# Count loads from GpSimd's queue, work moved out of the output attention's preparation, and first missing-edge tiles loaded ahead of a branch

## The chip, the cores and the metric

The kernel runs on 1 core of one Trainium2 chip. Its time is the device time of one execution, in microseconds (us); three runs of the kernel before took 2191.27, 2193.19 and 2195.49 us, median 2193.19 us. Engines are named as the profile names them: PE multiplies matrices, DVE is the vector engine, ACT the scalar engine with its function tables, POOL is GpSimd, and SP issues transfers. Each engine runs its own instructions in the order that was fixed when the program was built. A transfer that SP or POOL issues waits in that engine's order too (the profile writes SPq, POOLq).

## The reference

Four graph layers run one after the other on 4096 nodes of 64 features with a dense 0/1 adjacency of 4096 x 4096. Each layer gets the normalised, rectified features `h` and adds its output to `x`.

```
# layer 0: eight attention heads, then one "output attention" over their joined result
e_o   = leaky_relu(o1[:, None] + o2[None, :], 0.2)
att_o = softmax(where(mask, e_o, -9e15));   out = tanh(att_o @ Who)
# layer 1: hyperbolic attention, for every pair of nodes
adj_att = sigmoid(left[:, None] + right[None, :] + b) * adj
support = einsum('ij,ijd->id', adj_att, logmap(x_i, x_j))
# layer 2: mean over neighbours, a dense layer, rows scaled to length 1
# layer 3: the last 100 neighbours of each row, with weights 0.5 ** (number of neighbours behind)
rank = cumsum(adj != 0, axis=1);  w = mask * where(pos > 0, 0.5 ** (k - pos), 0);  out = w @ support + bias
```

## The kernel before, in words

Nodes are 32 blocks of 128 (`NB` = 32, `P` = 128). The adjacency is held as one byte per edge in DRAM (`mask_d`), written once from the float input during the attention heads, and loaded again by each later stage. The stages, with their place in the profiled execution:

- **Heads** (to about 937 us). Each of 8 heads runs over 2 halves of the targets. At the end of heads 3 and 7, `finish_unit` (from line 1660) goes over four groups: four transposes into PSUM, a copy by ACT into a slot of `h` (`hT`, line 1714), eight small products (L1720), an addition into `who` by DVE (L1731). All four groups use one slot, `by_g[:, 3]`. `h` and `by_g` are the same memory.
- **Output attention, preparation** (about 950 to 985 us). First constants of layer 1 are made (lines 1743 to 1768: three small loads by POOL and 11 instructions of one column on DVE), and POOL clears the tile `MOV` (L1777, 128 x 4096 bf16), of which later three rows are filled from DRAM (L1868). Then maxima of `who` are reduced (L1918 to L1935), joined over partitions by POOL (`omax`, L1166), and from these the value tiles `YB`, `YC`, `YD` are made. The sum over nodes, `wsum` (L1985, on DVE), feeds the mean value, and the last instruction of the preparation is `prepared` (L2006). Most of this stands in `in_order()`, which keeps DVE, ACT and PE in the order of the program text.
- **Output attention, four units u of 1024 targets** (to 1184 us). For each of 8 values of q, SP loads a mask tile `mo` (L2074, 512 KB, 3 buffers), DVE writes its complement and POOL stores it to DRAM (`noedge`, L2079), ACT takes signs (L1200), DVE forms the masked tiles B and C (L1206, L1214), and PE multiplies them (L2097). From u = 1 on, DVE also works on layer 1's nodes of the unit before.
- **A branch** (L2192, `values_load`) that sends unusual data to a slow path. What stands inside the branch isn't mixed with what stands ahead of it.
- **Pairs of layer 1** (about 1206 to 1785 us). `weights_of` (from line 2217) loads a tile `nm` of missing edges (L2221, 256 KB, 4 buffers), PE multiplies it (L2228) and then `MOV` (L2231), ACT takes the sigmoid. PE forms distances (L2259) in between.
- **Layer 2** (about 1785 to 1945 us). Two halves of 8 mask tiles `m2` (L2623, 1 MB, 3 buffers); POOL also copies `cat` (L2578) for each group of 512 nodes.
- **Layer 3** (about 1945 to 2185 us). Four units u; for each of 8 values of q a mask tile `m3` (L2690, 512 KB, 3 buffers), of which each of 4 blocks goes through PE (L2697, L2705), ACT (L2714) and PE again (L2679). A unit's sums are copied out of PSUM (L2724), half by DVE and half by ACT, before the next unit's sums may start. POOL stores the output (L2739).

Beside these runs a check of the input that is spread over the stages: `count_odd` (line 946) loads 1 MB of the float adjacency into a tile `raw` (L949, 2 buffers) and counts on DVE the entries that are neither 0 nor 1 (L950). It is called 64 times: 16 times in the output attention (q = 0, 2, 4, 6 of each unit), 11 times in layer 2, and 37 times in layer 3 (12, 9, 8 and 8 in its units). All 64 loads are issued by SP, in one queue with `mo`, `m2` and `m3`. A load waits in SP's order for its `raw` buffer, and what stands behind it on SP waits with it.

The order on each engine comes from a scheduler that goes by priorities in the order of the program text and by its own estimate of when things are ready. It may move a load or a count ahead of other work. `issue_after` and `behind` keep what is in their block behind a given instruction. The measured order shows that a `raw` load is not held by them (two were issued at 937 and 953 us, ahead of `prepared` at 980 us); the count on DVE is.

Of the kernel before, what the change touches and what calls it, by code (L numbers as in the profile page):

```python
# [9 lines left out]
F32 = mybir.dt.float32  # L10
BF16 = mybir.dt.bfloat16
# [5 lines left out]
U8 = mybir.dt.uint8  # L17
AF = mybir.ActivationFunctionType
ALU = mybir.AluOpType
AX = mybir.AxisListType  # L20
# [4 lines left out]
P = 128  # L25
N = 4096
NB = N // P
D = 64
G = 512
NG = N // G  # L30
GB = G // P
# [7 lines left out]
PROJ_EPS = 0.004  # L39
# [12 lines left out]
HW = N // 2  # L52
NS = HW // G
# [777 lines left out]
def kernel(  # L831
# [24 lines left out]
    nc = tc.nc  # L856
    NH, F, O = W_sp.shape[0] + W_int.shape[0], W_sp.shape[1], W_sp.shape[2]
# [10 lines left out]
    ctx = ExitStack()  # L868
# [74 lines left out]

        return col.unsqueeze(2).to_broadcast([P, col.shape[1], width])

    def count_odd(pool, c):

        raw = pool.tile([P, HW], F32, name="raw", tag="raw", bufs=2)
        nc.sync.dma_start(raw, adjT[c % NB * P : (c % NB + 1) * P, c // NB * HW : (c // NB + 1) * HW])  # L949
        nc.vector.scalar_tensor_tensor(  # L950
            raw, raw, 0.0, raw, ALU.is_gt, ALU.not_equal, accum_out=bad[:, c : c + 1]
        )
# [83 lines left out]
    with ExitStack() as l0:  # L1036
# [403 lines left out]
        with ExitStack() as ha:  # L1440
# [34 lines left out]
            for hf in range(2):  # L1475
# [9 lines left out]
                for hd in range(NH):  # L1485
# [174 lines left out]
                    def finish_unit(hf=hf, hd=hd, ev=ev, fme=fme):  # L1660
# [50 lines left out]
                            return  # L1711
                        c = hd // 4
                        for bq in range(NS):
                            hT = by_g[:, 3]
                            transpose_to(
                                hT, [num[:, bq * GB + b, :] for b in range(GB)], P, ps, nc.scalar.copy
                            )
                            pw = ps.tile([P, GB, D + 2], F32, name="pwho", tag="misc")
                            for b in range(GB):
                                nc.tensor.matmul(  # L1720
                                    pw[:, b, :],
                                    lhsT=hT[:, b * P : (b + 1) * P],
                                    rhs=rho[:, c, :],
                                    start=True,
                                    stop=True,
                                )
# [13 lines left out]
        lq = ctx.enter_context(tc.tile_pool(name="l1", bufs=1))  # L1740
        KA = D + 2

        def scalar_tile(name):
            return lq.tile([P, 1], F32, name=name)
# [4 lines left out]
        nc.vector.reciprocal(sqc, rabs)  # L1749
        nc.vector.tensor_tensor(cc, rt, rt, ALU.mult)  # L1750
        nc.vector.reciprocal(cc, cc)
        c2, m2c, p2c, m4c, cneg, maxn, hrow = (
            scalar_tile(n) for n in ("c2", "m2c", "p2c", "m4c", "cneg", "maxn", "hrow")
        )
        nc.vector.tensor_tensor(c2, cc, cc, ALU.mult)
        nc.vector.tensor_scalar(m2c, cc, -2.0, None, ALU.mult)
        nc.vector.tensor_scalar(m4c, cc, -4.0, None, ALU.mult)
        nc.vector.tensor_scalar(p2c, cc, 2.0, None, ALU.mult)
        nc.vector.tensor_scalar(cneg, cc, -1.0, None, ALU.mult)
        nc.vector.tensor_scalar(maxn, rabs, 1.0 - PROJ_EPS, None, ALU.mult)  # L1760
        nc.vector.tensor_scalar(hrow, rabs, 0.5, None, ALU.mult)
        wab = lq.tile([P, 2, D], F32, name="wab")
        nc.gpsimd.dma_start(
            wab.rearrange("p s d -> p (s d)"),
            w_att.rearrange("k o -> (k o)").unsqueeze(0).to_broadcast([P, 2 * D]),
        )
        bt = scalar_tile("bt")
# [9 lines left out]
        nc.gpsimd.memset(MOV, 0.0)  # L1777

        def layer1_nodes(bs, work, augs):

# [93 lines left out]
        with ExitStack() as ob:  # L1874
# [42 lines left out]
            for i, bs in enumerate(halves):  # L1917
                nc.vector.tensor_reduce(mx[:, i, 0:1], tcol[:, bs], AX.X, ALU.max)  # L1918
                nc.vector.tensor_reduce(mx[:, i, 1:2], tcol[:, bs], AX.X, ALU.min)
                nc.vector.tensor_reduce(mx[:, i, 2:3], vals[:, bs], AX.XY, ALU.max)  # L1920
                nc.vector.tensor_reduce(mx[:, i, 3:4], vals[:, bs], AX.XY, ALU.min)
            with in_order():

                pr = ps.tile([NB, P], F32, name="pro", tag="misc")
# [60 lines left out]
                nc.vector.tensor_reduce(wsum, vals.rearrange("p b d -> p d b"), AX.X, ALU.add)  # L1985
# [24 lines left out]
                None,  # L2010
                ALU.mult,
            )

            def finish_unit(u, evs):

# [44 lines left out]
            for u in range(4):  # L2060
# [133 lines left out]
    def pairs_fast(es, VT):  # L2194
# [10 lines left out]
        with ExitStack() as ss:  # L2205
# [11 lines left out]
            def weights_of(src, tgt):  # L2217


                nm = work.tile([P, GB, G], U8, name="nm", tag="nm", bufs=4)  # L2220
                nc.sync.dma_start(  # L2221
                    nm, noedge_d[src][tgt // NS][:, :, (tgt % NS) * G : (tgt % NS + 1) * G]
                )
# [237 lines left out]
    def layers_fast(es, wide, *sums):  # L2461
# [211 lines left out]
        for u in range(4):  # L2673
# [14 lines left out]
            for q in range(NQ):  # L2688
                m = work.tile([P, JT, HO2], U8, name="m3", tag="m3", bufs=3)
                nc.sync.dma_start(m, mask_d[q][u // 2][:, :, hs])  # L2690
                for t in range(JT):
# [142 lines left out]
```

## Time and profile before

| what | value |
|---|---|
| runs | 2191.27, 2193.19, 2195.49 us; median 2193.19 us |
| profiled execution | 2194.35 us; its span 2192.6 us |
| mean granted clock of PE | 0.933 |
| busy | PE 1923.9 us, DVE 1765.8, ACT 1623.2, POOL 84.7 |
| counts (L950) | 64 x about 2.29 us on DVE, 70.2 us of DVE idle time ahead of them, waiting for `raw` |
| `raw` loads | 64 x 1024 KB, median 6.6 us from issue to landing |

The profiled execution stands 1.2 us above the median of the runs. A row of a table by stage gives the stretch, its length, for each engine its busy time and (x the number of instructions), then the clock granted to PE as a share of full speed, the mean busy share of the 16 DMA engines, and the GB/s that they moved. A line of a timeline gives start, length, engine, line, operation, output <- input with shapes, and in brackets how long the engine had been idle and what ended that. A line of waits gives who waited, at which line, for whom, the total, how often, and the longest.

### The profile page before, as it was taken

Reading aid. Unit: us, or ns where it says so; the run is one execution under the profiler, and the core shown is the slowest. Engines: PE = TensorE matmul, PEld = TensorE weight load, DVE = VectorE, ACT = ScalarE, POOL = GpSimd, SP = SyncE. Lnnn points to the kernel's source line nnn. Section 1 sums busy time; section 2 is a strip of 40 time slices with the busy share of each in tenths; the row PEclk is TensorE's granted clock in tenths of the full one; section 3 lists DMA queues with packets and bytes.
Section 4 is the critical chain, followed back from the end, with each engine's and each line's share of the span. In section 5 each row is a group of like instructions: output and inputs, shape, how many; then the busy total and the mean of one; then the engine's idle time right before and its main releaser. Section 6 shows DMA issues by size and latency. Waiting matters only on the chain.

```text
span 2192.6 us, 43992 instructions
## 1 busy us (share of the span) xinstructions
PE 1923.9 (88%) x19276; PEld 865.5 (39%) x19276; DVE 1765.8 (81%) x2330; ACT 1623.2 (74%) x1402; POOL 84.7 (4%) x124
## 2 busy tenths in 40 slices
PE   4989989999999999949997699999999968989878
PEld 3444444444444444423443233333333323444222
DVE  6689989997898899978986799998989987634554
ACT  4678878997798799847885778888888862146546
POOL 1000100000000000011110000000000000000000
PEclk8999999999999999959998799999999988879979
DMA  9945554343111111049751111011011133824885
GB/s 112 187 95 93 98 87 113 126 180 130 45 45 45 45 50 50 2 158 333 249 174 68 35 29 29 25 34 39 25 29 34 34 110 133 307 65 139 304 301 200
DMA packets 117008, 239.01 MB, mean 109 GB/s; under 512 B 11059, under 2 KB 84003, under 8 KB 102051
## 3 DMA queue, kind: packets, MB, share of 16 engines
q1 hardware_dynamic: 101990, 192.92, 25.6%
q0 software_dynamic: 14816, 43.18, 11.0%
q8 instruction: 153, 2.51, 0.5%
q14 instruction: 49, 0.40, 0.1%
HBM read 245.34 MB, written 49.46 MB: 134 GB/s over the span
## 4 chain that ended last, share of the span: by engine, by line
PE 30%; DVE 14%; issue 12%; ACT 6%; DMA 2%; POOL 0%; POOLq 0%; SPq 0%; DVEq 0%; ACTq 0%
PE accj L2292 6%; PE pu L2259 3%; PE acco L2097 3%; PE pl L2228 2%; PE pf L2330 2%; PE pl L2231 2%; DVE at L2281 2%; PE accC L1536 2%; DMA mo<-edges 2%; PE nacc L2628 1%; ACT sg L2215 1%; PE accB L1536 1%; ACT xt L2215 1%; DVE at L2286 1%; ACT root L2215 1%
## 5 line engine op out<-in xcount | busy, mean ns | idle before, releaser
L1200 ACT ACTIVATE st<-srow,nt 128x2048 int8<-128x2048 f32 x352 | 682.8, 1994 | 77.1 <-DVE B L1206 76.3
L1206 DVE TENSOR_TENSOR B<-st,mres 128x1024 int32<-128x1024 int32 x256 | 311.9, 1221 | 65.8 <-PE accC L1536 41.3
L1536 PE MATMUL accB<-B,ybh 128*32 128x512 fp8e4 x3072 | 338.3, 384 | 15.6 <-DVE B L1206 15.6
L1536 PE MATMUL accD<-B,ybh 128*32 128x512 fp8e4 x2048 | 300.7, 386 | 22.2 <-DVE h L1652 22.2
L1536 PEld LDWEIGHTS <-ybh 128*32 128x32 bf16 (+1 forms) x6656 | 197.1, 98 | 237.4 <-issue 75.6
L1536 PE MATMUL accC<-B,ycn 128*32 128x512 fp8e4 x2272 | 266.8, 379 | 1.2 <-issue 1.2
L1536 PE MATMUL accC<-mres,ych 128*32 128x512 fp8e4 x2272 | 266.9, 380 | 0.0
L1536 PE MATMUL accL<-B,ybh 128*32 128x512 fp8e4 x1536 | 220.2, 391 | 4.7 <-DVE h L1656 4.5
L2292 PE MATMUL accj<-sg,who 128*64 128x512 f32 (+1 forms) x512 | 199.6, 619 | 17.8 <-DVE sg L2333 6.9
L1536 PEld LDWEIGHTS <-ych 128*32 128x32 f16 x4096 | 168.4, 98 | 114.5 <-issue 9.0
L1194 DVE TENSOR_SCALAR st<-srow,nt 128x2048 uint8<-128x2048 f32 x160 | 205.5, 1285 | 2.5
L950 DVE SCALAR_TENSOR_TENSOR raw<-raw 128x2048 f32<-128x2048 f32 x64 | 146.2, 2287 | 70.4 <-DMA raw<-in_adj_dram 70.2
L2215 ACT ACTIVATE sg<-pl,rb 128x512 f32<-128x512 f32 x256 | 163.3, 684 | 48.3 <-PE pl L2231 44.0
L2292 PE MATMUL acci<-sg,who 128*64 128x512 f32 (+1 forms) x512 | 199.1, 618 | 0.0
L2714 ACT ACTIVATE w3b<-pv 128x1024 int16<-128x1024 f32 x128 | 130.0, 1023 | 82.9 <-PE pv L2705 81.8
L1200 ACT ACTIVATE st<-srowo,nto 128x1024 int8<-128x1024 f32 x128 | 137.9, 1138 | 25.4 <-DVE B L1206 25.4
L2259 PE MATMUL pu<-XAf,LDf 66*128 66x512 f32 x288 | 146.8, 612 | 7.1 <-DVE at L2266 4.7
L1536 PE MATMUL accC<-C,ych 128*32 128x512 fp8e4 x1824 | 145.7, 388 | 1.2 <-DVE C L1214 1.2
L1214 DVE TENSOR_TENSOR C<-B,mres 128x1024 int32<-128x1024 int32 x114 | 139.6, 1225 | 3.6
L1536 PEld LDWEIGHTS <-ycn 128*32 128x32 f16 x2272 | 107.4, 97 | 63.7 <-issue 2.9
L2266 DVE TENSOR_SCALAR at<-pu 128x512 f32<-128x512 f32 x144 | 95.3, 684 | 20.0 <-PE pu L2259 19.2
L2228 PE MATMUL pl<-nm,noid 128*128 128x512 fp8e4 x256 | 99.8, 390 | 10.5 <-ACT sg L2215 8.9
(497 smaller groups left out, 3132.2 us busy)
## 6 DMA issues: line engine op xcount, KB each, us to landing
raw<-in_adj_dram SPq DMA_DIRECT2D x64, 1024.0 KB, 6.6
mo<-edges SPq DMA_DIRECT2D x32, 512.0 KB, 4.3
noedge<-nmo POOLq DMA_DIRECT2D x32, 512.0 KB, 4.2
nm<-noedge SPq DMA_DIRECT2D x64, 256.0 KB, 3.0
m<-edges SPq DMA_DIRECT2D x16, 1024.0 KB, 4.8
m<-edges SPq DMA_DIRECT2D x32, 512.0 KB, 6.2
srow<-srow_d SPq DMA_DIRECT2D x15, 1024.0 KB, 6.8
mres<-in_adj_dram POOLq DMA_DIRECT2D x8, 1024.0 KB, 35.9
```

Source lines behind the costliest of these rows:

```text
L950: nc.vector.scalar_tensor_tensor(raw, raw, 0.0, raw, ALU.is_gt, ALU.not_equal, accum_out=bad[:, c : c + 1])
L1194: nc.vector.tensor_scalar(st[:, i, :].bitcast(U8), srow, negs[:, i : i + 1], EDGE, ALU.is_gt, ALU.mult)
L1200: nc.scalar.activation(st[:, i, :], srow, AF.Sign, bias=negs[:, i : i + 1], scale=-1.0)
L1206: nc.vector.tensor_tensor(B.bitcast(I32), st.bitcast(I32), edges.bitcast(I32), ALU.bitwise_and)
L1214: nc.vector.tensor_tensor(C.bitcast(I32), B.bitcast(I32), edges.bitcast(I32), ALU.bitwise_xor)
L1536: ins = nc.tensor.matmul(acc[k * O : (k + 1) * O, :], lhsT=values, rhs=moving(k), start=start, stop=stop,)
L2215: tc.keep_in_program_order(nc.scalar.activation(*args, **kw))
L2228: nc.tensor.matmul(pl, lhsT=noid, rhs=nm[:, b, :].bitcast(F8), start=True, stop=False)
L2259: nc.tensor.matmul(pu, lhsT=LD[:, j * P : (j + 1) * P], rhs=XA[:, grp(gi)], start=True, stop=True,)
L2266: nc.vector.tensor_scalar(at[:, b, :], pu, UMIN, None, ALU.max)
L2292: nc.tensor.matmul(acc[r : r + n, :], lhsT=XQ[:, src, cols], rhs=w, start=start, stop=stop)
L2714: nc.scalar.activation(w, pv, AF.Relu)
```

## The change

Five edits:

1. `count_odd` takes the queue that issues its load. The calls in layers 2 and 3 give `nc.gpsimd`; those in the output attention stay on SP.
2. Fewer counts stand in the output attention (q = 0, 3, 5 of each unit: 12), and more in layer 3 (14, 9, 9 and 9 in its units: 41). Layer 2 keeps 11.
3. The constants of layer 1 and the clearing of `MOV` move behind `prepared`. The sum over nodes becomes five additions on POOL, in `h`'s memory, ahead of the preparation.
4. The first three tiles of missing edges are loaded ahead of the branch, from a pool of their own that stands until the end of the kernel. `sel` moves into the free half of the distances' tile `LD_all`.
5. The four groups of the heads' `finish_unit` use four slots for `hT`.

```diff
-    def count_odd(pool, c):
+    def count_odd(pool, c, queue=nc.sync):
         raw = pool.tile([P, HW], F32, name="raw", tag="raw", bufs=2)
-        nc.sync.dma_start(raw, adjT[...])
+        queue.dma_start(raw, adjT[...])
...
-                            hT = by_g[:, 3]
+                            hT = by_g[:, bq]
...
-        rt, rabs, sqc, cc = (scalar_tile(n) for n in ("rt", "rabs", "sqc", "cc"))
-        nc.gpsimd.dma_start(rt, r_in.unsqueeze(0).to_broadcast([P, 1]))
-        nc.vector.scalar_tensor_tensor(rabs, rt, -1.0, rt, ALU.mult, ALU.max)
...
-        nc.gpsimd.dma_start(bt, b_att.unsqueeze(0).to_broadcast([P, 1]))
...
         MOV = lq.tile([P, N], BF16, name="MOV")
-        nc.gpsimd.memset(MOV, 0.0)
...
+            wsum = h[:, halves[0]]
+            nc.gpsimd.tensor_tensor(wsum, vals[:, halves[0]], vals[:, halves[1]], ALU.add)
+            for n in (8, 4, 2, 1):
+                nc.gpsimd.tensor_tensor(wsum[:, 0:n], wsum[:, 0:n], wsum[:, n : 2 * n], ALU.add)
             with in_order():
...
-                wsum = spool.tile([P, D], F32, name="wsum")
-                nc.vector.tensor_reduce(wsum, vals.rearrange("p b d -> p d b"), AX.X, ALU.add)
                 pss = ps.tile([P, D], F32, name="psso", tag="misc")
-                nc.tensor.matmul(pss, lhsT=ones, rhs=wsum, start=True, stop=True)
+                nc.tensor.matmul(pss, lhsT=ones, rhs=wsum[:, 0], start=True, stop=True)
...
+            with behind(prepared.ins):
+                rt, rabs, sqc, cc = (scalar_tile(n) for n in ("rt", "rabs", "sqc", "cc"))
+                nc.gpsimd.dma_start(rt, r_in.unsqueeze(0).to_broadcast([P, 1]))
...
+                nc.gpsimd.memset(MOV, 0.0)
...
-                    if q % 2 == 0:
+                    if q in (0, 3, 5):
                         with behind(prepared.ins):
                             count_odd(work, next(todo))
...
+    nmp = ctx.enter_context(tc.tile_pool(name="nmp", bufs=4))
+    missing = {}
+    def load_missing(src, tgt):
+        nm = nmp.tile([P, GB, G], U8, name="nm", tag="nm")
+        nc.sync.dma_start(nm, noedge_d[src][tgt // NS][:, :, (tgt % NS) * G : (tgt % NS + 1) * G])
+        missing[src, tgt] = nm
+    for src, tgt in ((0, 0), (0, 1), (1, 0)):
+        load_missing(src, tgt)
     nc.vector.tensor_scalar(pm, pc, MIN_NORM, None, ALU.max)
...
-                nm = work.tile([P, GB, G], U8, name="nm", tag="nm", bufs=4)
...
+                if (src, tgt) not in missing:
+                    load_missing(src, tgt)
+                nm = missing.pop((src, tgt))
...
-        sel = lp.tile([P, NB * O], BF16, name="sel")
+        sel = LD_all.bitcast(BF16)[:, NB * P : NB * (P + O)]
...
-                            count_odd(work, next(todo))
+                            count_odd(work, next(todo), nc.gpsimd)
...
-                    if (j % 4 == 1 or j == 31 and u == 1) if u else j % 5 and j > NB // 2:
+                    if (j % 4 == 1 or j == 31) if u else j > NB // 2 + 1:
                         with tc.issue_after(valued[-1].ins):
-                            count_odd(work, next(todo))
+                            count_odd(work, next(todo), nc.gpsimd)
```

More of the change, by code (lines that the diff above doesn't have):

```diff
@@ L944, in over @@
         return col.unsqueeze(2).to_broadcast([P, col.shape[1], width])
-    def count_odd(pool, c):
+    def count_odd(pool, c, queue=nc.sync):
         raw = pool.tile([P, HW], F32, name="raw", tag="raw", bufs=2)
-        nc.sync.dma_start(raw, adjT[c % NB * P : (c % NB + 1) * P, c // NB * HW : (c // NB + 1) * HW])
+        queue.dma_start(raw, adjT[c % NB * P : (c % NB + 1) * P, c // NB * HW : (c // NB + 1) * HW])
         nc.vector.scalar_tensor_tensor(
@@ L1741 @@
         KA = D + 2
-        def scalar_tile(name):
-            return lq.tile([P, 1], F32, name=name)
-        rt, rabs, sqc, cc = (scalar_tile(n) for n in ("rt", "rabs", "sqc", "cc"))
-        nc.gpsimd.dma_start(rt, r_in.unsqueeze(0).to_broadcast([P, 1]))
-        nc.vector.scalar_tensor_tensor(rabs, rt, -1.0, rt, ALU.mult, ALU.max)
[L1749 to L1767, printed above, removed]
-        nc.gpsimd.dma_start(bt, b_att.unsqueeze(0).to_broadcast([P, 1]))
         a, pc, pm, pinv, pabs, left, nrb = (
@@ L2012, with scalar_tile @@
             )
+            with behind(prepared.ins):
+                def scalar_tile(name):
+                    return lq.tile([P, 1], F32, name=name)
+                rt, rabs, sqc, cc = (scalar_tile(n) for n in ("rt", "rabs", "sqc", "cc"))
+                nc.gpsimd.dma_start(rt, r_in.unsqueeze(0).to_broadcast([P, 1]))
+                nc.vector.scalar_tensor_tensor(rabs, rt, -1.0, rt, ALU.mult, ALU.max)
+                nc.vector.reciprocal(sqc, rabs)
+                nc.vector.tensor_tensor(cc, rt, rt, ALU.mult)
+                nc.vector.reciprocal(cc, cc)
+                c2, m2c, p2c, m4c, cneg, maxn, hrow = (
+                    scalar_tile(n) for n in ("c2", "m2c", "p2c", "m4c", "cneg", "maxn", "hrow")
+                )
+                nc.vector.tensor_tensor(c2, cc, cc, ALU.mult)
+                nc.vector.tensor_scalar(m2c, cc, -2.0, None, ALU.mult)
+                nc.vector.tensor_scalar(m4c, cc, -4.0, None, ALU.mult)
+                nc.vector.tensor_scalar(p2c, cc, 2.0, None, ALU.mult)
+                nc.vector.tensor_scalar(cneg, cc, -1.0, None, ALU.mult)
+                nc.vector.tensor_scalar(maxn, rabs, 1.0 - PROJ_EPS, None, ALU.mult)
+                nc.vector.tensor_scalar(hrow, rabs, 0.5, None, ALU.mult)
+                wab = lq.tile([P, 2, D], F32, name="wab")
+                nc.gpsimd.dma_start(
+                    wab.rearrange("p s d -> p (s d)"),
+                    w_att.rearrange("k o -> (k o)").unsqueeze(0).to_broadcast([P, 2 * D]),
+                )
+                bt = scalar_tile("bt")
+                nc.gpsimd.dma_start(bt, b_att.unsqueeze(0).to_broadcast([P, 1]))
+                nc.gpsimd.memset(MOV, 0.0)
             def finish_unit(u, evs):
@@ L2217, in weights_of @@
             def weights_of(src, tgt):
-                nm = work.tile([P, GB, G], U8, name="nm", tag="nm", bufs=4)
-                nc.sync.dma_start(
-                    nm, noedge_d[src][tgt // NS][:, :, (tgt % NS) * G : (tgt % NS + 1) * G]
-                )
+                if (src, tgt) not in missing:
+                    load_missing(src, tgt)
+                nm = missing.pop((src, tgt))
                 sg = work.tile([P, GB, G], F32, name="sg", tag="sg", bufs=6)
```

## The prediction

> **What bounds the kernel now.** I read the page first: the slices show no engine that is full throughout, and the DMA row is full in two places only, the output attention and layer 3. All edits but one lie there. So I took the busy time by stage:
>
> ```profile
> core 0: us, PE busy (x) PEld busy (x) DVE busy (x) ACT busy (x) POOL busy (x), PEclk, DMA share, GB/s
> 969.00:1036.00 67.00, 56.55 (x335) 22.41 (x336) 60.00 (x92) 48.86 (x53) 6.43 (x9) 0.90 0.71 261
> 1036.00:1086.00 50.00, 45.52 (x316) 20.96 (x316) 45.28 (x97) 40.27 (x44) 5.00 (x7) 1.00 0.77 256
> 1086.00:1138.00 52.00, 47.01 (x312) 20.87 (x310) 45.19 (x95) 42.68 (x47) 6.42 (x9) 0.93 0.57 195
> 1138.00:1184.00 46.00, 44.78 (x319) 21.98 (x317) 30.60 (x75) 34.87 (x46) 3.56 (x5) 1.00 0.35 118
> ...
> 2008.00:2066.00 58.00, 50.97 (x216) 16.14 (x216) 32.71 (x34) 34.86 (x36) 1.57 (x2) 0.91 0.79 276
> 2066.00:2138.00 72.00, 56.58 (x212) 16.92 (x210) 38.73 (x38) 32.54 (x34) 1.50 (x2) 0.81 0.89 307
> 2138.00:2182.00 44.00, 42.96 (x204) 14.35 (x202) 20.82 (x24) 33.28 (x34) 1.86 (x3) 1.00 0.66 239
> ```
>
> The first four rows are the output attention's units, the last three layer 3's u = 1, 2, 3. Each group does equal PE work per row. The fastest row is PE's floor: 46 us a unit in the output attention, 44 in layer 3. Above the floor are 21 + 4 + 6 us and 14 + 28 us. In layer 3 the waits of u = 2 say why:
>
> ```profile
> DVE raw L950 <- DMA raw<-in_adj_dram: 31.1, 15, 4.5
> ...
> PE pv L2705 <- DMA m<-edges: 8.6, 5, 3.0
> ```
>
> PE waits for `m3`, and the granted clock falls to 0.81 over the stretch (1.00 in u = 3, where PE does not wait). SP's own order shows why `m3` is late:
>
> ```profile
> 2072.81 4.17 SPq L949 DMA_DIRECT2D raw<-in_adj_dram  x2
> 2077.07 0.52 SPq L2690 DMA_DIRECT2D m<-edges  x1
> 2081.24 5.26 SPq L949 DMA_DIRECT2D raw<-in_adj_dram  x2
> 2086.59 0.52 SPq L2690 DMA_DIRECT2D m<-edges  x1
> ```
>
> Two `raw` loads, each waiting for its buffer, then one `m3`: one mask per 9.5 us, where the 44 us floor uses one per 5.5 us.
>
> **Part 1, preparation.** Timeline around the maxima, then the sum:
>
> ```profile
> 954.51 2.41 DVE L1932 TENSOR_SCALAR mx<-mx 128x2 f32<-128x2 f32 x1
> ...
> 953.36 3.54 POOL L1777 MEMSET MOV<- 128x4096 bf16 x1
> 957.22 0.40 POOL L1166 PARTITION_ALL_REDUCE omax<-m  x1 [0.33 <-DVE nto L1938]
> ...
> 976.18 3.98 DVE L1985 TENSOR_REDUCE wsum<-who 128x64 f32<-128x2048 f32 x1
> ```
>
> An instruction on two columns takes 2.41 us and ends with the MEMSET (953.36 + 3.54 = 956.90): POOL's clearing held DVE. With 0.15 us for it (the later one-column instructions), the maxima are ready near 954.9 and `omax` could start 2.3 us earlier. But POOL now has the additions ahead of it in the program: 16+8+4+2+1 = 31 pairs of 64 columns = 1984 columns. The trace has no addition on POOL. Its copy of 256 columns takes 0.40 us and its cast of 512 takes 0.61, so 0.8 to 1.2 ns a column; with one such read per operand I estimate 2.4 to 5.3 us for five. From 952.0 (last addition to `who`) they end at 954.4 to 957.3; `omax` gains between 2.3 and -0.1 us. I take 0, by the larger end: two operands.
>
> On DVE `wsum` goes: -3.98 us, and DVE was busy 5.00 of 5 us from 970 to 980, so it counts in full. The 11 constants cost nothing today (they run at 957.1 to 957.9 while DVE waits for `omax`); behind `prepared` they cost 11 x about 0.07 us of spacing = +0.8. The moved MEMSET can hold DVE again: 0 to +2.3 us, and the three loads on POOL (0.55 us each) sit ahead of it; constants are first used at about 1040, so only their place on DVE costs. I take 0, since most DVE work there is additions and masks and not the form that was held. Sum -3.2, from -5.5 to +2.
>
> **Part 2, four counts fewer in the output attention.** Each is 2.37 us on DVE (2.29 and 0.08 for reading the sum) and 1.05 MB. SP takes `raw` early: 9 of 16 counts ran ahead of 1036, 4 in u = 1, 3 in u = 2, none in u = 3. DVE is full through much of 1050 to 1120, DMA at share 0.93 to 1.04 through 985 to 1030. Removing one per unit for u = 0, 1, 2 gives 3 x 2.4 = -7.2 us; the fourth I count as hidden. All 31 us above the floor less 17 us of first wait for B bound it at -14; zero if the scheduler puts other counts in their place.
>
> **Part 3, missing edges.** PE idles 1.03 us for `nm` at 1211.38, behind four distance products that end at 1210.34. The first product can move up to the landing of `MOV`, issued 1206.74 and 1.4 us at the least on its way (`lr_d`'s landing), so -1.0 to -3.2 us; I take -1.5. The loads are three SP instructions ahead of L1867; SP is idle there (44 us of waiting). Next late is `MOV`.
>
> **Part 4, four `hT` slots.** The copy that would wait for the slot waits for its transpose instead ("2.97 <-PE tr"), so 0; if PE's order changes, three gaps of 0.7 us: -2.1. `sel` in the distances' tile: cleared by POOL in 1.01 + 0.28 us at 1793, hidden behind the node steps to 1812; 0.
>
> **Part 5, layer 2.** Of 6.8 us of PE waits for `m2`, all but 0.4 come ahead of 1856, where when no waiting `raw` load stands ahead of it on SP; nothing to win, 0. On POOL a `cat` copy (0.40 us, on the chain of each group) now queues behind a `raw` load that waits for its buffer; a buffer turn of up to 8 us. Two of eight copies hit by 3 us: bound +6, other side -4 (the clock falls to 0.50 to 0.59 at 1900 to 1910).
>
> **Part 6, layer 3.** Here bytes decide. From 2008 to 2138 it moves 276 x 58 + 307 x 72 = 38.1 MB. Of the four added counts three stand ahead of u = 3: 41.3 MB. At today's mean 293 GB/s that is 141 us, +11. With `m3` in its own queue it need not sit behind two `raw`, and the gaps of the DMA (shares 0.79 and 0.89) can fill. Full share means 307 / 0.89 = 345 GB/s: 120 us, -10. I take 0.93, between u = 2 and the full stretches of 985 to 1030: 321 GB/s, 128.6 us, **-1.4**. The ninth count of u = 3 fits: 44 us at 4.7 us from count to count. A separate queue is worth it by these rows, landing of a 512 KB mask in u = 2 and in the output attention without `raw`:
>
> ```profile
> m<-edges SPq DMA_DIRECT2D x10, 512.0 KB, 6.3
> ...
> mo<-edges SPq DMA_DIRECT2D x6, 512.0 KB, 3.8
> ```
>
> The Trainium skill speaks against this. *DMA: Bandwidth & Descriptors*, section "Issuing engines are not separate DMA queues", says that all issuing engines end on the same 16 DMA engines, so that another issuer saves only the time to issue. By it part 6 would be +11 and the whole about 2193; no row here has `raw` in POOL's queue to test it. *SBUF — State Buffer*, section "SBUF: two separate sides", warns that a DMA issued by GpSimd starves while DVE runs in a two-port mode. The trace agrees in the heads, where one POOL issue took 2.06 us in place of 0.62, beside DVE's TENSOR_SCALARs (L1194, L1522); in layer 3 the stores on POOL took 0.75 to 0.80 us beside counts, so by this row the rule costs nothing there.
>
> **Sum** -3.2 - 7.2 - 1.5 + 0 + 0 - 1.4 = -13.3 us against the profiled 2194.35, 1.2 us above the median: **2181 us**.
>
> **Rivals.** (a) *Layer 3 opens up*: DMA full, -10 in place of -1.4: 2172; for it, PE's 42 us above the floor; against, only two `raw` buffers. (b) *DMA keeps today's pace*: +11 in place of -1.4: 2193. (c) *The slower side: POOL's turn is longer.* 37 counts take 2008 to 2175, 4.5 us each; PE ends 7 us after the last. POOL's issue takes 0.75 us, SP's 0.33; shared by two buffers that is +0.2, so 41 x 4.7 = 193 us against 167 + 7: +19, the rest -11.9: about 2201. It decides once a count takes over 174 / 41 = 4.2 us, and PE is then held at L2724 behind counts. Against it: u = 3 runs 4.7 us a count with PE never waiting. (d) *Counts are hoisted again, omax takes the wait*: parts 1 and 2 give -2: 2190.
>
> **Numbers.** Forecast 0.42, (a) 0.14, (b) 0.20, (c) 0.16, (d) 0.08. A measurement of this kernel can tell about 0.2% (4.4 us). Faster: forecast and (a), 0.56. Same: half of (b), a fifth of (c), all of (d): 0.21. Slower: 0.23. The range runs from (a) with most of part 2's bound (-12 in place of -7.2) taken too, 2167, to (c), 2201; the bounds left out lie beyond these and need several at once.
>
> **What would show it.** `wsum` gone from DVE and `prepared` about 4 us earlier; L1932 near 0.15 us; `omax` near 957. Units of 48 to 50 us at u = 1, 2. Layer 3: no PE wait for `m3`, DMA above 315 GB/s. I am wrong if u = 1 and 2 of layer 3 still take 130 us with DVE waiting for `raw`, if PE waits at L2724, or if `cat` is late in layer 2.

## The result

The changed kernel takes 2381.85 us (median of 4 runs, 2380.77 to 2386.14), the kernel before 2194.34 us beside it (4 runs, 2191.27 to 2198.88): 1.086 times as long, 95% interval 1.083 to 1.088. Forecast were 2181 us and a range of 2167 to 2201. The profiled execution of the changed kernel has a span of 2379.0 us, that of before 2192.6: 186.4 us to be found.

I cut both spans at six landmarks that any trace shows (each taken at its start): the last addition to `who`, the issue of `lr_d` (the end of the output attention), the last `VT` (the end of the pairs), the last cast of counts in layer 2, the first `ev` copy of layer 3, the end.

| us | before | changed | difference |
|---|---|---|---|
| start to the last addition to `who` | 951.5 | 953.2 | +1.7 |
| output attention, to `lr_d` | 253.1 | 253.4 | +0.3 |
| pairs, to the last `VT` | 587.8 | 757.1 | **+169.3** |
| layer 2, to the last cast of counts | 136.3 | 123.3 | -13.0 |
| layer 2's last groups and layer 3's first unit | 82.9 | 97.6 | +14.7 |
| layer 3, from the first `ev` copy to the end | 181.0 | 194.4 | +13.4 |

Nine tenths of the loss lie in the pairs, to which the forecast gave -1.5 us. The waits of the changed kernel over the pairs (waiting engine and line, what it waits for, us in all, times, longest):

```profile
ACT sg L2229 <- PE pl L2244: 194.4, 129, 3.3
...
PEld L2241 <- DMA nm<-noedge: 88.4, 36, 3.6
...
PE pl L2241 <- DMA nm<-noedge: 60.4, 33, 3.0
```

and of the kernel before:

```profile
PE pl L2228 <- DMA nm<-noedge: 1.0, 1, 1.0
```

The two lines of the changed kernel mustn't be added: the 33 waits of TensorE's products, 60 us, lie inside the 36 waits of its weight load (PEld), 88 us. Before there was one wait, of 1.0 us. The transfer is no slower, by the list of DMA issues (KB each, median us to landing; 3.0 before):

```profile
nm<-noedge SPq DMA_DIRECT2D x64, 256.0 KB, 3.1
```

So the loads are issued too late. SyncE's own waits over the same stretch, first the changed kernel, then the kernel before:

```profile
SPq L2170 <- PE pl L2244: 542.6, 55, 60.0
SPq L2170 <- DMA nm<-noedge: 150.1, 60, 3.1
```

```profile
SPq L2221 <- PE pl L2231: 508.6, 58, 45.6
```

The line with the DMA is new: 60 of the loads wait for the landing of an earlier load, 2.5 us each, and then for TensorE to have read it. One turn of it in the changed kernel's timeline (start, us, engine and line; the SyncE row is the first of three loads that it puts together):

```profile
1305.97 0.57 PE L2241 MATMUL pl<-nm,noid 128*128 128x512 fp8e4 x1 [0.22 <-issue]
1306.57 13.66 SPq L2170 DMA_DIRECT2D nm<-noedge  x3
1309.43 0.10 PEld L2241 LDWEIGHTS <-noid 128*128 128x128 bf16 x1 [3.31 <-DMA nm<-noedge]
1309.44 0.39 PE L2241 MATMUL pl<-nm,noid 128*128 128x512 fp8e4 x1 [2.68 <-DMA nm<-noedge]
```

The last product on one tile ends at 1306.54, the next load is issued 0.03 us later, and TensorE goes on only when it has landed. Four buffers are declared; one turns. The traces let us count it: in the changed kernel 61 of the 64 loads are issued once the products on the load just ahead of them are done, before the change once the products on the fourth load ahead are done.

Waits are only a part of the loss. The stretch of the pairs as a whole, first before, then changed (same columns as the table in the prediction):

```profile
1204.50:1792.30 587.80, 529.41 (x2320) 198.35 (x2320) 523.18 (x499) 492.59 (x443) 1.45 (x4) 0.95 0.10 29
1206.60:1963.70 757.10, 627.09 (x2281) 230.31 (x2320) 535.21 (x527) 499.40 (x448) 2.91 (x7) 0.83 0.08 23
```

TensorE's idle time grows from 58 to 130 us, by 72; its busy time grows from 529 to 627 us, by 98, for the same products (39 of their records are missing in the second row). Of the 72 us, 59 are the waits for missing edges. The granted clock is 0.83 in place of 0.95. Not every product takes longer: one on missing edges takes 472 ns in place of 390, a distance product (`pu`) 754 in place of 610, while those of the sums (`acci`, `accj`) stay at 615 to 625 (618).

The units of the output attention and of layer 3 in the changed kernel (same columns again):

```profile
971.00:1044.00 73.00, 54.84 (x337) 22.38 (x338) 63.81 (x120) 49.94 (x60) 14.55 (x17) 0.88 0.69 249
1044.00:1093.00 49.00, 45.42 (x317) 20.79 (x317) 45.72 (x101) 42.15 (x47) 6.41 (x9) 1.00 0.64 220
1093.00:1139.00 46.00, 45.09 (x316) 20.61 (x315) 38.36 (x90) 41.93 (x47) 5.69 (x8) 1.00 0.56 182
1139.00:1184.00 45.00, 43.31 (x306) 20.60 (x306) 29.73 (x70) 32.66 (x43) 3.56 (x5) 1.00 0.31 108
2181.00:2231.00 50.00, 47.03 (x221) 16.49 (x226) 27.81 (x29) 36.06 (x37) 6.88 (x12) 1.00 0.82 290
2231.00:2289.00 58.00, 46.91 (x205) 15.91 (x208) 30.41 (x32) 33.24 (x33) 8.40 (x15) 0.85 0.87 305
2289.00:2344.00 55.00, 45.00 (x198) 15.54 (x202) 28.69 (x29) 32.31 (x32) 7.87 (x14) 0.91 0.81 280
2344.00:2379.00 35.00, 1.97 (x8) 1.78 (x8) 16.20 (x19) 0.00 (x0) 4.02 (x7) 0.50 0.47 160
```

The output attention's second and third units shrink from 50 and 52 to 49 and 46 us (48 to 50 were forecast), but the first starts 2 us later and takes 6 us more. In layer 3 TensorE's three units shrink together (from 58 + 72 + 44 = 174 to 50 + 58 + 55 = 163 us), and a row almost without TensorE follows: 35 us, in which VectorE first finishes the counts (the last ends at 2366.8).

### The profile page after: what moved, and what is told of

It is laid out like the page before. It is cut to its first block, busy times and chain, and to the rows that moved or that the text cites. A ratio compares the mean times of both kernels' runs of the same rounds, so it can differ in the third digit from the quotient of the medians.

```text
span 2379.0 us, 43942 instructions
## 1 busy us (share of the span) xinstructions
PE 2009.4 (84%) x19220; PEld 900.1 (38%) x19276; DVE 1765.5 (74%) x2329; ACT 1629.4 (68%) x1404; POOL 118.5 (5%) x181
## 4 chain that ended last, share of the span: by engine, by line
PE 30%; issue 12%; DVE 11%; DMA 7%; ACT 6%; POOL 1%; POOLq 0%; DVEq 0%; ACTq 0%
PE accj L2305 5%; DMA nm<-noedge 4%; PE pl L2241 4%; PE pu L2272 3%; PE pf L2343 3%; PE pl L2244 2%; PE acco L2101 2%; DVE at L2294 2%; PE acci L2305 2%; DMA raw<-in_adj_dram 2%; PE accC L1536 2%; ACT st L1200 1%; DVE at L2299 1%; ACT xt L2229 1%; PE nacc L2641 1%
## 5 line engine op out<-in xcount | busy, mean ns | idle before, releaser
L2229 ACT ACTIVATE sg<-pl,rb 128x512 f32<-128x512 f32 x256 | 167.3, 685 | 212.5 <-PE pl L2244 194.4
L2305 PE MATMUL accj<-sg,who 128*64 128x512 f32 (+1 forms) x512 | 204.5, 625 | 11.9 <-DVE VT L2363 5.9
L2272 PE MATMUL pu<-XAf,LDf 66*128 66x512 f32 x288 | 183.4, 754 | 34.1 <-DVE at L2279 30.3
L2241 PE MATMUL pl<-nm,noid 128*128 128x512 fp8e4 x256 | 120.7, 472 | 64.7 <-DMA nm<-noedge 60.4
L1200 ACT ACTIVATE st<-srowo,nto 128x1024 int8<-128x1024 f32 x128 | 137.3, 1137 | 35.7 <-DVE B L1206 26.0
L2319 DVE TENSOR_TENSOR sg<-sg,at 128x2048 f32<-128x2048 f32 x36 | 82.2, 2285 | 95.3 <-ACT sg L2229 95.3
```

The costliest lines, as they stand in the source:

```text
L1200: nc.scalar.activation(st[:, i, :], srow, AF.Sign, bias=negs[:, i : i + 1], scale=-1.0)
L2229: tc.keep_in_program_order(nc.scalar.activation(*args, **kw))
L2241: nc.tensor.matmul(pl, lhsT=noid, rhs=nm[:, b, :].bitcast(F8), start=True, stop=False)
L2272: nc.tensor.matmul(pu, lhsT=LD[:, j * P : (j + 1) * P], rhs=XA[:, grp(gi)], start=True, stop=True,)
L2305: nc.tensor.matmul(acc[r : r + n, :], lhsT=XQ[:, src, cols], rhs=w, start=start, stop=stop)
L2319: nc.vector.tensor_tensor(w, w, F_, ALU.mult)
```

## The experiments

The theories ahead of the first four runs: **H**, the three tiles filled ahead of the branch keep their buffers while the branch runs; **R**, something else in the change slows the pairs; **P**, the pool's place ahead of the branch is enough.

### no_early_pool: the fourth edit undone

```
-    nmp = ...; load_missing(...) for three tiles, ahead of the branch
+    nm = work.tile([P, GB, G], U8, name="nm", tag="nm", bufs=4)   # inside, as before
```

> The changed kernel with one edit undone: the missing edges (`nm`) come again from the pool inside the branch, with four buffers, and no load stands ahead of the branch. Theory H (held buffers): the three tiles loaded ahead of the branch are never given back inside it, so one buffer of four turns, and each load waits for the products on the one before; that costs 169 us of the 187 between `lr_d` and the last `VT`. Then this kernel takes 2382 - 169 = about 2211 us (2203 to 2219), and the stage from `lr_d` to the last `VT` takes 588 us as before. Rival R (the stage is slowed by something else that the change moved: the scratch of the node sum, the clearing, the place of `sel`): the stage stays above 700 us and the time above 2330.

2228.7 us, 1.016 times before (1.011 to 1.021); pairs 590.4 us. R falls, H stands for the pairs. But the time is 18 us above the 2211 that I expected and 10 above the range: I had taken the 13 us that the changed kernel wins in layer 2 as a gain of its own, and here it is gone (137.3 us to the last cast of counts). It was work slipped forward: VectorE's busy time over the pairs was 535.2 us in the changed kernel (523.2 before) and over the next stretch 84.8 (97.8 before), so node steps of layer 2's start had run in the idle time of the pairs. The pairs lost 169 us, and 13 of them came back there. Another 6 us of the miss lie in layer 3 (200.3 us, in the changed kernel 194.4).

### before_plus_early: the fourth edit alone

The kernel before with the pool, the three loads and `sel` moved as in the change.

> The kernel before with only the early loads of the missing edges: the pool ahead of the branch with four buffers, three loads ahead of it, and `sel` in the distances' tile, which makes room for the pool. Theory H: 2194 + 169 = about 2363 us, stage from `lr_d` to the last `VT` about 757 us. Rival R: about 2194, the stage near 588.

2340.9 us in one run; pairs 759.4 us, then 120.9 us to the last cast (136.3 before). The edit alone makes the loss. The sum missed by 22 us, 15 of them the time given back in layer 2, 7 in layer 3 (174.4 us, at a granted clock of 0.93 in place of 0.89).

### early_one, early_two, early_none: how many buffers are held

```
-    for src, tgt in ((0, 0), (0, 1), (1, 0)):
+    for src, tgt in ((0, 0), ):          # early_one; early_two: two; early_none: no loop
         load_missing(src, tgt)
```

> The changed kernel with one load ahead of the branch in place of three; pool, buffers and place stay. Theory H: three of four buffers turn, so most of the 169 us comes back: 2211 to 2250 us. Rival P (the pool's place ahead of the branch makes each load wait, however many are loaded early): about 2380. Rival R: about 2380.

> The changed kernel with the pool ahead of the branch, but no load ahead of it: all 64 loads are issued inside. Theory H: nothing is held, four buffers turn, about 2211 us (2203 to 2219), as with the pool inside. Rival P (place of the pool): about 2380. Rival R: about 2380.

> The changed kernel with two loads ahead of the branch in place of three, so that two of four buffers should turn. Theory H with its price: 169 us over 61 loads is 2.8 us a load, about the landing of 3.1 us, which one turning buffer leaves bare. Two buffers hide it behind the products of the other tile: 2225 to 2240 us, as with one load ahead (2225). Rival L (each held buffer costs its share): about 2300.

One run each: early_one 2225.0 us, early_none 2234.9, early_two 2223.0; pairs 588.8, 591.2 and 589.3. P falls (the pool stands ahead of the branch in all three), and so does L (each held buffer costs its share). early_none misses its range by 16 us, for the same reason as no_early_pool: it has neither the 13 us of layer 2 (136.3 there) nor the changed kernel's layer 3 (197.5). early_two's time lies 2 us below its range. With two loads ahead, the same waits as above are nearly gone:

```profile
PEld L2241 <- DMA nm<-noedge: 4.3, 9, 0.7
...
PE pl L2241 <- DMA nm<-noedge: 0.2, 1, 0.2
```

So the cost is a step and no slope. The order of loads and products in the traces gives the number of buffers that turn: 61 loads are issued behind the products on the fourth load ahead in early_none, the third in early_one, the second in early_two and the first in the changed kernel. With 4, 3 and 2 the landing of about 3 us hides behind the products on other tiles; with one it doesn't, and TensorE's weight load stands for it 36 times, 2.5 us each. The 169 / 61 = 2.8 us a load of the expectation is close to the landing by chance: it is a mean over these waits and the slower products.

### layer2_sp: layer 2's counts back on SyncE's queue

```
-   count_odd(work, next(todo), nc.gpsimd)      # layer 2 only, from no_early_pool
+   count_odd(work, next(todo))
```

> The run no_early_pool with layer 2's eleven `raw` loads back on SyncE's queue; layer 3's stay on GpSimd's. Theory C (copies behind loads): on GpSimd a `cat` copy stands behind `raw` loads that wait for VectorE, one node group of layer 2 comes a whole turn late, and layer 3's first maxima end 14 us later (97 us from the last cast of counts to the first `ev` copy, 83 before). Then 2229 - 14 = 2215 us (2207 to 2222), with 83 us in that stretch. Rival D (the group is late because the counts themselves stand elsewhere on VectorE, whatever the queue, or the clock): 2224 to 2234, 95 us or more.

2217.1 us, 1.011 times before (1.007 to 1.015), with 82.9 us in that stretch. The size is as theory C had it; its mechanism is not in the trace. In no_early_pool's timeline of GpSimd the late `cat` copy waits for TensorE's transpose, not behind a load:

```profile
1896.35 0.53 POOL L949 DMA_DIRECT2D raw<-in_adj_dram  x1 [3.78 <-DVE raw L950]
1903.88 0.40 POOL L2582 COPY cat<-h 128x256 f32<-128x256 f32 x1 [7.00 <-PE tr L995]
```

What is late lies on VectorE, between the first group's `zt` and the second group's `cat` (no_early_pool):

```profile
1877.98 2.29 DVE L950 SCALAR_TENSOR_TENSOR raw<-raw 128x2048 f32<-128x2048 f32 x1 [1.99 <-DMA raw<-in_adj_dram]
1880.20 0.08 DVE L950 DVE_READ_ACCUMULATOR raw<-raw 128x1 f32 x1
1880.20 0.41 DVE L2598 TENSOR_REDUCE nrm<-sq 128x4 f32<-128x256 f32 x1
...
1889.45 2.29 DVE L950 SCALAR_TENSOR_TENSOR raw<-raw 128x2048 f32<-128x2048 f32 x1 [1.74 <-DMA raw<-in_adj_dram]
1891.67 0.08 DVE L950 DVE_READ_ACCUMULATOR raw<-raw 128x1 f32 x1
1891.67 0.17 DVE L980 RECIPROCAL ln_var<-ln_var 128x4 f32<-128x4 f32 x1
```

A count waits 1.99 us for its `raw`, and the group's reduction stands behind it although its input is there. Four such counts stand in that piece, with 6.5 us of waiting; in the kernel before three stand there, none of them waiting. The piece takes 23.9 us, before 13.7, in layer2_sp 13.7: 10 of the 14 us. So with the other queue the counts stand elsewhere on VectorE, one more of them in this piece, and they stand ahead of node steps with their data still on the way. Rival D was wrong in that the queue decides, and right about the place.

### counts_as_before and all_sp: the number of counts, and the queue

counts_as_before is no_early_pool with the conditions of before (16 in the output attention, 37 in layer 3); all_sp is no_early_pool with every `raw` on SyncE's queue.

> The run no_early_pool with the counts shared out as in the kernel before (16 in the output attention, 11 in layer 2, 37 in layer 3), all of layer 2's and 3's still on GpSimd's queue. Theory T (the turn of the counts sets layer 3's end): 42 counts at 4.4 us stand behind the last maxima; with five fewer the tail of 38 us behind ScalarE's last `ev` copy falls to about 18, and the output attention gets 5 to 10 us longer: 2214 to 2222 us. Rival G (GpSimd's queue is slow by itself, the number does not matter): the tail stays above 30 us and the time is 2229 to 2240.

> The run no_early_pool with all counts back on SyncE's queue, but shared out as changed (12, 11, 41). Theory T: the number of counts, not the queue, makes layer 3's tail, so only layer 2's 14 us come back, and layer 3 with its tail takes 200 us as on GpSimd's queue (170 + 11 before, and four counts more at 4.5 us): about 2214 us. Rival G (the queue makes it): layer 3 and its tail fall to about 181 to 185, time 2196 to 2200. Rival M (masks late behind two `raw` loads, as before): layer 3 at 210 us or more, 2225.

2215.6 us (1.012 times before, 1.008 to 1.016) and 2207.1 us (1.007, 1.004 to 1.009). From layer 3's first `ev` copy to the end, by queue and number:

| us | 37 counts | 41 counts |
|---|---|---|
| SyncE's queue | 181.0 (before) | 190.7 (all_sp) |
| GpSimd's queue | 180.1 (counts_as_before) | 200.3 (no_early_pool) |

Each is one profile, and no_early_pool is the longest of the seven kernels with 41 counts on GpSimd's queue (194.4 to 200.3). So four counts cost 14 to 20 us there and 10 on SyncE's queue, where T expected 20. At 37 counts the queues are alike, so counts_as_before's G falls. At 41 all_sp lies between T (200) and its own G (181 to 185). layer2_sp differs from all_sp by layer 3's queue alone; it takes 9 us more in layer 3 (199.6) and 10 us more in the median of the runs.

From count to count layer 3 takes 4.56 us before, 4.58 in the changed kernel, 4.62 in counts_as_before, 4.73 in no_early_pool and 4.47 in all_sp. Two `raw` buffers, each taken by a landing of 6.5 us and a count of 2.4, turn once in about (6.5 + 2.4) / 2 = 4.5 us. The turn also holds the 10 us between the queues at 41 counts: 40 x (4.73 - 4.47) = 10.4 us. Why it is longer on GpSimd's queue there and not in the changed kernel stays open. In all_sp TensorE still waits 17.6 us for `m3` and ends behind the counts; with GpSimd's queue these waits are gone (0.8 us or less in all seven), TensorE has its last sums before the counts are done, and the counts set the end.

### layer3_queue_alone: the sixth part by itself

The kernel before with `nc.gpsimd` as the queue of layer 3's 37 loads and nothing else.

> The kernel before with one thing changed: layer 3's 37 `raw` loads come from GpSimd's queue. Theory T (the turn of the counts sets the end once the masks are on time): from the first `ev` copy to the end 180 us as in counts_as_before (156 + 24), against 181 before: within 3 us of before (2189 to 2195). Rival G (the queue helps by itself, the masks of u = 1 and 2 come in time): 173 us, 2184 or less.

2200.4 us, 1.0036 times before (1.0020 to 1.0052). This run's G (the queue helps by itself) falls. T's range is missed by 5 us, and the profile can't say why: the profiled execution was the fastest of eleven (2189.1 us) and has 176.9 us in layer 3. That stays open.

### sum_on_dve, sum_after_max and sum_behind_max: the node sum

sum_on_dve is no_early_pool with the old `nc.vector.tensor_reduce` for `wsum`. The other two start from two_more_in_output (below).

> The run no_early_pool with the sum over the nodes back on VectorE as one instruction in its old place; clearing and constants stay behind `prepared`. Theory W (GpSimd's additions hold the all-reduce of `omax`, which ends 12 us later than before): `omax` starts within 6 us of the last addition to `who` (18 now), and the output attention ends 5 to 9 us earlier: 2220 to 2224 us. Rival B (the output attention is bound by its transfers and gives it back): within 2 us of 2229.

2224.8 us (1.014 times before, 1.011 to 1.018); the output attention takes 248.9 us, against 252.3 to 257.3 in the seven kernels with twelve counts and the sum on GpSimd. `omax` starts 5.7 us behind the last addition to `who` (17.1 in the changed kernel), so W stands, though the gain in time is small: the runs of the two kernels overlap (2215.5 to 2227.4 and 2225.3 to 2231.7). In the changed kernel GpSimd shows why; the bracket is its idle time ahead of an instruction:

```profile
951.28 0.73 POOL L2083 DMA_DIRECT2D noedge<-nmo  x1 [17.27 <-ACT h L996]
958.80 2.83 POOL L1895 TENSOR_TENSOR h<-who 128x1024 f32<-128x1024 f32 x1 [6.79 <-issue]
970.27 0.38 POOL L1166 PARTITION_ALL_REDUCE omax<-m  x1 [8.64 <-issue]
977.69 1.26 POOL L1897 TENSOR_TENSOR h<-h 128x512 f32<-128x512 f32 x1 [7.04 <-issue]
```

The five additions are 5.8 us of work (2.83 + 1.26 + 0.73 + 0.57 + 0.41). But ahead of the first, ahead of `omax` and ahead of the second GpSimd idles 7 to 9 us with nothing that the view names (1.6 us of the first gap are the wait for `who`). The view by line names it: an instruction that the timeline leaves out, MODIFY_POOL_CONFIG, stands in GpSimd's stream at each of the three changes, at 952.0, 961.8 and 970.6 us. For the additions (how many, ns shortest/median/longest, us of the first and last start):

```profile
L1895 POOLq MODIFY_POOL_CONFIG  x2: 108/108/108, 952.0 to 952.0; - x2
...
L1897 POOLq MODIFY_POOL_CONFIG  x2: 83/83/83, 970.6 to 970.6; - x2
```

The kernel before has it in two places only, at 1.9 and 16.2 us, where the waits that follow end with something else (a DMA, and VectorE at 37 us). All kernels with the additions ahead of `omax` show the three gaps, 6.8 to 9.9 us each; no kernel without additions on GpSimd does.

```
     m3 = col_maxs(m3, 4, "omax", hp)
     ...
+    nc.vector.tensor_copy(wsum[:, 0, 0:1], td[:, 0:1])   # sum_behind_max only
+    the five additions                                   # both
```

> The run two_more_in_output with the node sum on GpSimd again, but its five additions behind the all-reduce of `omax` in place of ahead of it. In the changed kernel the additions took GpSimd from 953.6 to 970.3 (the first, ahead of `omax`) and from 970.7 to 982.4 (the other four), about 28 us in all by these bounds. Theory W: here `omax` starts about 6 us behind the last addition to `who` as before, VectorE is rid of 3.98 us, but the additions end near 957 + 28 = 985, some 8 us behind the place where `psso` needs them; it gives 0, between -4 and +4 us against two_more_in_output (2185.7). Rival S (the additions take 2.4 to 5.3 us, as the prediction had it, and only waited for something ahead of `omax`): they end by 963, `prepared` comes 4 us earlier, 2182.

> The run two_more_in_output with the node sum on GpSimd, its first addition now waiting for a value that VectorE works out from `omax`, so that all five stand behind the all-reduce. Theory K (each change between additions and all-reduce costs GpSimd about 7 us, the additions are quick): `omax` starts about 6 us behind the last addition to `who`; one gap of about 7 us stands ahead of the first addition, none ahead of the second; the five end 13 to 15 us behind `omax`, in time for `psso`; VectorE is rid of 3.98 us: 2180 to 2185 us against 2185.7. Theory A (the additions themselves are slow): a gap ahead of the second addition too, the five end 25 us or more behind `omax`, `psso` waits: 2188 or more.

sum_after_max told nothing apart: written behind the all-reduce, the first addition was still scheduled ahead of it, with the same three gaps (7.27, 8.08, 6.88 us), and the time was 2197.4 us (1.0021, 1.0005 to 1.0036), the output attention 263.2. In sum_behind_max a real dependence holds it back:

```profile
958.19 0.39 POOL L1166 PARTITION_ALL_REDUCE omax<-m  x1 [0.33 <-DVE nto L1910]
968.33 2.36 POOL L1914 TENSOR_TENSOR h<-who 128x1024 f32<-128x1024 f32 x1 [9.75 <-DVE pzo L1935]
970.65 0.86 POOL L2084 DMA_DIRECT2D noedge<-nmo  x1
971.53 4.09 POOL L1916 TENSOR_TENSOR h<-h 128x512 f32<-128x512 f32 x4
```

One gap is left, ahead of the first addition, and `omax` starts 5.7 us behind the last addition to `who`, as before. K stands, with 9.75 us where 7 were expected (the profile puts the end of it down to VectorE; MODIFY_POOL_CONFIG stands at 958.5) and the additions done 17 us behind `omax`, not 13 to 15. The time is 2187.9 us (0.998, 0.996 to 1.000), 3 us outside K's range and no better than with the sum on VectorE. The Trainium skill describes such a gap: *GPSIMD Engine Reference*, section "2.1 Instruction dispatch", says that the first call of a freshly loaded GpSimd routine pays about 6 us (5.95 measured there) for bringing in its code, with no instruction visible in the profile. The page measured it from MODIFY_POOL_CONFIG, less the wait for an event. That instruction stands at the gaps here, 6.8 to 8.6 us in the changed kernel. The page speaks of a first call; here the gap comes back at every change. That it is the loading of code is the page's word: the rows show the instruction and the idle time, not what fills it.

### more_in_output and two_more_in_output: counts the other way

Counts cost 5 us each in layer 3 (on GpSimd's queue) and little in the output attention. So: sum on VectorE, one early load, layer 2 on SyncE's queue, layer 3 on GpSimd's, and

```
-    if q in (0, 3, 5):                       # 12 in the output attention, 41 in layer 3
+    if q % 2 == 0 or q == 5:                 # more_in_output: 20 and 33
+    if q % 2 == 0 or q == 5 and u < 2:       # two_more_in_output: 18 and 35
```

> The counts moved the other way: 20 in the output attention, 11 in layer 2 on SyncE's queue, 33 in layer 3 on GpSimd's queue; the node sum on VectorE, one early load of the missing edges, the rest as changed. By stages against the kernel before: output attention 248.9 + 8 x 1.3 = 259.3 (before 253.1): +6; pairs +1; layer 2 0; layer 3 bound by TensorE again, 156 + 12 = 168 (before 181.0): -13. Sum -6, about 2184 us (2178 to 2190). Rival Y (the output attention pays a whole 2.4 us on VectorE for each count): 268 there, +15 in all, 2192 to 2196.

> As more_in_output, with 18 counts in the output attention and 35 in layer 3. Stages: output attention 248.9 + 6 x 1.3 = 256.7: +3.6; layer 3 two counts shorter than with 37 (180.1), at 4.4 to 5 us each: 170, -11; pairs +1. Sum -6, about 2184 us (2178 to 2190). Rival Y: output attention 263: +10, about 2190.

2187.7 us, 0.9978 times before (0.9961 to 0.9995), and 2185.7 us, 0.9963 (0.9948 to 0.9978). Both beat the changed kernel, and the kernel before by 0.2 and 0.4%. Y falls: the output attention takes 253.2 us with 20 counts and 249.3 with 18 (forecast 259.3 and 256.7). Layer 3 takes 172.6 and 174.5 (forecast 168 and 170).

## Why the prediction was wrong

**The step that failed is part 3**, "so -1.0 to -3.2 us; I take -1.5. The loads are three SP instructions ahead of L1867". It costed where the first three loads go and not what they leave behind for the other 61. The diff moves the pool out of the branch and fills three of its four buffers there; the runs show that those three don't turn inside the branch, so that each of 61 loads waits for the products on the one ahead: pairs +169 us. The gain itself shows among the kernels that have the other changes: pairs 588.8 and 589.3 us with one and two loads ahead, 591.2 and 590.4 with none (before 587.8). The bound "-1.0 to -3.2" had no upper side, though the profile of before held what a rough one needs: 64 loads that land in 3.0 us each.

**Part 1** (-3.2): right that `wsum` leaves VectorE and that L1932 loses its hold; the same instruction, now L1908, takes 0.17 us:

```profile
956.19 0.17 DVE L1908 TENSOR_SCALAR mx<-mx 128x2 f32<-128x2 f32 x1
```

Wrong that `omax` gains 0: it starts 13 us later (970.3 against 957.2). The additions' work was sized about right (2.4 to 5.3 us forecast, 5.8 measured), though the range doesn't follow from its source: 0.8 to 1.2 ns over 1984 columns is 1.6 to 2.4 us for one read and 3.2 to 4.8 for two. The three changes between additions and other work, 22 us of idle time, were not in the sum. Nothing in the trace of before shows what one costs.

**Part 2** (-7.2): the second and third units shrink by 1 and 6 us, but the first unit, late and 6 us longer, eats it; the stage is +0.3. A count less there is worth under the 2.4 us that I took: with the sum on VectorE 12, 18 and 20 counts take 248.9, 249.3 and 253.2 us, and with it on GpSimd 12 and 16 take 254.3 and 259.4 (1.3 us each, from kernels that spread by 5 us with the same counts).

**Part 5** (0, bound +6): +14.7, 14.0 of it given back by layer2_sp (against no_early_pool). I looked at GpSimd's `cat` copies; the loss is on VectorE, whose order of counts and node steps changed with the queue.

**Part 6** (-1.4): +13.4. "Here bytes decide" is the wrong step: the rates of the three units were 276, 307 and 239 GB/s and are 290, 305 and 280, and the turn of two `raw` buffers decides. Rival (c) had this, "41 x 4.7 = 193 us" and +19, and its sign: 41 counts at 4.58 us, TensorE held at the `ev` copy behind counts. Its reason, a longer turn because GpSimd issues more slowly, does not show in the changed kernel (4.58 us against 4.56; an issue of `raw` takes 0.53 us, not 0.75). In layer 3 of the changed kernel TensorE waits for VectorE's half of that copy at three units (us in all, times, longest):

```profile
PE pn L2742 <- DVE ev L2737: 26.3, 3, 10.9
```

At the last unit:

```profile
2342.14 0.58 ACT L2737 COPY ev<-sacc 128x512 f32<-128x512 f32 x1 [0.47 <-PE sacc L2692]
2348.16 2.29 DVE L950 SCALAR_TENSOR_TENSOR raw<-raw 128x2048 f32<-128x2048 f32 x1 [1.65 <-DMA raw<-in_adj_dram]
2350.38 0.69 DVE L2737 COPY ev<-sacc 128x512 f32<-128x512 f32 x1
```

ScalarE copies its half at 2342.14; VectorE's half comes 8 us later, behind two counts. The aim of the edit was met: `m3` lands in 4.8 us (6.2 before) and TensorE no longer waits for it. The rule that the prediction quoted from *DMA: Bandwidth & Descriptors*, that another issuer doesn't add transfer, agrees with these rates: the highest is 307 GB/s before and 305 now. Of the other rule quoted there (*SBUF — State Buffer*, section "SBUF: two separate sides") these runs show nothing: the loads on GpSimd were issued in 0.53 us beside the counts.

**Part 4** (0): nothing in the runs speaks against it; the `hT` slots were not tried by themselves.

The prediction's opening says that the DMA row is full in two places only; the row is also at 9 tenths in its first two slices, up to 110 us, which no edit touches.

Without part 3 the forecast would still have been wrong: no_early_pool is 39 us slower than before, 48 above the forecast.

## What to carry to other kernels

When loads are moved ahead of a branch or a loop, cost every later load of that pool too: count the buffers that can still turn inside, and compare the landing with the work on one tile. When counts, checks or other fillers share two buffers, multiply their number by the turn (landing plus use, over two) before adding any, and look at what stands behind them on their engine. A small job given to GpSimd between two of another kind can cost the changes of kind on top of its own length, here 22 us on top of 6; MODIFY_POOL_CONFIG in the view by line marks them.

## What was not expected of the hardware

- GpSimd idles 6.8 to 8.6 us at each change between additions and the all-reduce in the changed kernel, behind a MODIFY_POOL_CONFIG; between additions it doesn't, and between a clearing and the all-reduce it idles 0.33 us (before).
- The clearing of `MOV` (3.54 us on GpSimd) holds a two-column VectorE instruction for 2.41 us; with the clearing elsewhere it takes 0.17. In sum_on_dve, sum_behind_max and the two kernels with more counts in the output attention the clearing was scheduled ahead of `omax` again, though the program text has it behind `prepared`, and the same instruction took 2.40 or 2.41. So what the moved clearing gives by itself was not measured.
- A stage in which TensorE waits in short pieces ran at a lower granted clock, 0.83 in place of 0.95 over the pairs (no_early_pool), and a distance product took 754 ns in place of 619: of the 169 us, 72 are idle time of TensorE and 98 are slower products.
